# Gated delta rule in a decoder kernel: smaller TensorE tiles for the triangular inverse and the output, and eight steps in flight for five

## The chip, the cores and the metric

The kernel runs on one core of a Trainium2 chip, as one launch. The metric is the device time of that launch in microseconds (us). All data are float32. The engines are named as the profile names them: PE is TensorE's matmul, PEld its weight load, DVE is VectorE, ACT is ScalarE, POOL is GpSimd, SP is SyncE, which here issues DMAs.

## What is computed

A decoder of two layers works on 32 sequences of 64 tokens, 256 wide. Layer 0 has a decaying linear attention, a windowed cross attention and a feed-forward part; layer 1 has a gated delta rule, a cross attention and a mixture of 64 experts. The change lies in the delta rule alone. Cut to its core, with one chunk of 64 tokens per sequence (so that the running state of the reference is zero and drops out):

```
q, k, v   = silu(causal conv over 4 tokens of x @ w_qkv)      # 16 key heads, 32 value heads, 128 wide
q, k      = l2norm(q) * 128**-0.5, l2norm(k)
decay     = where(lower, exp(g_i - g_j), 0)
A         = where(strict, -(beta * k) @ k.T * decay, 0)       # 64 x 64 per sequence and head
T         = inverse of (I - A)                                # unit lower triangular
o         = where(lower, q @ k.T * decay, 0) @ (T @ (beta * v))
x         = x + (rmsnorm(o) * norm_w * silu(x @ w_z)) @ w_out
```

## The kernel before, in words

The delta rule is the stage in lines 711 to 1205. It works in 64 steps: 16 key heads by 4 groups of 8 sequences (512 tokens). Each step has two value heads, so 16 matrices A of 64x64. They lie in tiles of 128 partitions by 8 units by 64: two sequences on the two halves of the partitions, and eight units (four token tiles by two heads) along the free dimension.

A step s is made by these generators, each a stream of its own:

- `conv` (line 831): the projection pp (line 850), the causal convolution as one ACT and three DVE instructions (lines 854 and 859), and silu (864). It runs four times a step, for k, q and two halves of v.
- `decay` (867): one broadcast load per two steps, two POOL subtractions and additions per step, one exp.
- `matrices` (892): squares on POOL (903), their sums pn on PE (910), the products pk (943), and the masked matrices am (A transposed) and at (attention transposed) on DVE (951). It stores am to a DRAM buffer adram (957) and, for every second step, loads the 16x16 diagonal blocks from it as w, 512 blocks on 128 partitions by four (964).
- `value` (972): transposes v on PE (985) and scales it on ACT (989).
- `invert` (996): inverts the 16x16 blocks of two steps on DVE with 28 small instructions (1007, 1010), stores the inverses and their transposes in the DRAM buffer tudram (1016), and loads them as tu (1028): T and its transpose U, 64x64 with the four 16x16 diagonal blocks filled.
- `delta` (1055): completes the inverse in two levels, from blocks of 16 to 32 and from 32 to 64. First level: px = A T (am as the weights) on the left columns of each pair of blocks, a masked copy into xi (1085), ptu = T xi (U as the weights), a copy back into T (1090). Second level: a second px, and pm = T^T at (both in line 1067), a masked copy into the second xi (1097), a copy of pm to mt (1100), a last pm = xi^T mt for the right half, and its copy (1105). The helper `per_sequence` (1063) issues one 64x64 matmul per unit and sequence, so 16 in a block.
- `output` (1108): po, values times mt (1118), 16 matmuls with 64 rows and 128 weight columns; the square on ACT, the gate on DVE, the sum of squares pso on PE (1136), and the inverse root on POOL (1144).
- `gate` (1035): pz (1047) and silu. `project` (1148): py (1158), scaled and added to x on ACT, DVE and POOL (1165, 1167, 1169).

The order is written by a planner, `scheduled` (line 41). Each stream yields the engine and the time that it expects of its next piece; the planner takes the piece that could start first, and among those within 0.3 us of it the one whose stream stands first in the list (lines 1187 to 1195). "need" and "set" order pieces in the plan: conv needs the step five or six before to be done, and invert the step two pairs before. The number behind a stream is how many of its items may be open. "+" takes one of six PSUM banks, "-" gives it back, "c" means the two banks of conv, "t" a small tile shape. The plan fixes the order on every engine; the waits that the chip then makes come from the data and the buffers.

Of the kernel before, what the change touches and what calls it, by code (L numbers as in the profile page):

```python
# [23 lines left out]
LEVELS = (16, 32)  # L24
# [96 lines left out]
def decoder_kernel(ctx: ExitStack, tc: tile.TileContext, d, out):  # L121
# [589 lines left out]
    with tc.tile_pool(name="g1", bufs=1) as wp, tc.tile_pool(  # L711
# [6 lines left out]
        id64 = load(wp, d["c_id64"], [P, S], "id64")  # L718
        low = load(wp, d["c_low"], [P, S], "low")
        lvl = wp.tile([P, 2, S], U8, name="lvl")  # L720
# [4 lines left out]
        adram = [dp.tile([2, 2, 8, PITCH], FP, name=f"adram{i}") for i in range(2)]  # L725
        tudram = [dp.tile([2, 2, 2, 8, PITCH], FP, name=f"tudram{i}") for i in range(2)]
# [4 lines left out]
        xis = [[wp.tile([P, 8, S], FP, name=f"xi{l}{i}") for i in range(2)] for l in range(2)]  # L731
        for i in range(2):
            nc.sync.dma_start(out=wo16[i].rearrange("p o j e -> p o (j e)"), in_=d["c_wid"].rearrange("p (o x) -> p o x", o=2))
        for xs_ in xis:
            for t in xs_:
                nc.gpsimd.tensor_copy(t, over(id64, 8))
# [10 lines left out]
        with tc.tile_pool(name="g1l", bufs=1) as tmp:  # L747
            lvlf = load(tmp, d["c_lvl"].rearrange("p (l i) -> p l i", l=2), [P, 2, S], "lvlf")
# [68 lines left out]
        seqs = [slice(64 * n, 64 * n + 64) for n in range(2)]  # L817


        def load_weights(kh):  # L820
            wqkv = sb.tile([P, 2, 4, P], FP, name="wqkv", tag="wqkv")
            for i, at, n in ((0, kh, 1), (1, 16 + kh, 1), (2, 32 + 2 * kh, 2)):
                nc.sync.dma_start(
                    out=wqkv[:, :, i : i + n, :].rearrange("p k n e -> p k (n e)"),
                    in_=wsrc[:, :, at * P : (at + n) * P],
                )
            wz = load(sb, zsrc[:, :, kh * 256 : (kh + 1) * 256], [P, 2, 256], "wz")
            wo = load(sb, osrc[:, 2 * kh : 2 * kh + 2, :], [P, 2, D], "wo")
            weights[kh] = wqkv, wz, wo

        def conv(s, i):
# [3 lines left out]
            if i == first:  # L835
                yield "need", ("done", s - (5 if i == 2 or c == 0 else 6))
# [18 lines left out]
            yield "dve", 2.3, "-"  # L855
# [36 lines left out]
        def matrices(s):  # L892
# [55 lines left out]
            am = sb.tile([P, 8, S], FP, name="am", tag="am", bufs=6)  # L948
            at = sb.tile([P, 8, S], FP, name="at", tag="at", bufs=6)
# [6 lines left out]
            for n in range(2):  # L956
                nc.sync.dma_start(
                    out=adram[m % 2][j, n, :, : 64 * S].rearrange("u (r e) -> r u e", e=S), in_=am[seqs[n]]
# [3 lines left out]
            if j:  # L962
                w = sb.tile([P, 16, 16], FP, name="w", tag="w")
                nc.sync.dma_start(
                    out=w,
                    in_=adram[m % 2].rearrange("c n u (b x) -> (c n u b) x", b=4)[:, : 16 * S]
# [29 lines left out]
        def invert(m):  # L996
# [3 lines left out]
            yield "need", ("done", 2 * m - 4)  # L1000
# [14 lines left out]
            for o in range(2):  # L1015
                nc.sync.dma_start(
                    out=tudram[m % 2][o].rearrange("c n u (b x) -> (c n u b) x", b=4)[:, : 16 * S]
# [4 lines left out]
            for j in range(2):  # L1022
                yield "need", ("stored", m)
                yield "need", ("done", 2 * m + j - 4)
                tu = sb.tile([P, 2, 8, S], FP, name="tu", tag="tu", bufs=4)
                for n in range(2):
                    for o in range(2):
                        nc.sync.dma_start(
                            out=tu[seqs[n], o],
                            in_=tudram[m % 2][o, j, n, :, : 64 * S].rearrange("u (r e) -> r u e", e=S),  # L1030
# [24 lines left out]
        def delta(s):  # L1055

            kh, c = steps[s]
            yield "need", ("inverse", s)
            am, at = tokens.pop(s)
# [3 lines left out]
            def per_sequence(dst, lhsT, rhs):  # L1063

                for u in range(8):
                    for n in seqs:
                        nc.tensor.matmul(dst[n, u], lhsT[n, u], rhs[n, u], start=True, stop=True)  # L1067

            def columns(m, l):

                return m.rearrange("p u (b two c) -> p u b two c", two=2, c=LEVELS[l])[:, :, :, 0]

            def units(name, l):
                t = ps.tile([P, 8, S // 2], FP, name=name, tag="ps")
                return t.rearrange("p u (b c) -> p u b c", c=LEVELS[l])
# [5 lines left out]
            yield "pe", 0.65, "+t"  # L1081
            px = units("px", 0)
            per_sequence(px, am, columns(T, 0))
            yield "dve", 0.45, "-"
            nc.vector.copy_predicated(columns(xi[0], 0), columns(over(lvl[:, 0, :], 8), 0), px)
            yield "pe", 0.65, "+t"
            pt = units("ptu", 0)
            per_sequence(pt, U, columns(xi[0], 0))
            yield "act", 0.45, "-"
            nc.scalar.copy(columns(T, 0), pt)  # L1090
            yield "pe", 1.6, "++t"
            px = units("px", 1)
            per_sequence(px, am, columns(T, 1))
            pm = ps.tile([P, 8, S], FP, name="pm", tag="ps")
            per_sequence(pm, T, at)
            yield "dve", 0.45, "-"
            nc.vector.copy_predicated(columns(xi[1], 1), columns(over(lvl[:, 1, :], 8), 1), px)
# [3 lines left out]
            yield "pe", 0.65, "+t"  # L1101
            pm = ps.tile([P, 8, S // 2], FP, name="pm2", tag="ps")
            per_sequence(pm, xi[1], mt[:, :, S // 2 :])
            yield "act", 0.45, "-"
            nc.scalar.copy(mt[:, :, S // 2 :], pm)
            yield "set", ("weights", s)

        def output(s):

            yield "need", ("weights", s)  # L1110
            yield "need", ("gate", s)
            yield "need", ("value", s)
            mt, vs, eo = outs.pop(s), values.pop(s), factors.pop(s)[1]
            yield "pe", 1.0, "++t"
# [399 lines left out]
```

## Time and profile before

| | us |
|---|---|
| median of 8 runs | 3693.08 |
| lowest, highest | 3685.01, 3703.21 |
| the profiled execution | 3688.37 |
| its span, first to last instruction | 3686.7 |
| the stage: first pp (line 850) to end of last py (line 1158) | 934.1 to about 2597 |
| PE busy in the whole span | 3361.7 |
| mean granted clock of TensorE | 0.935 |

A line of the time line has the start, the length, the engine, the source line, the operation, the tiles (output, then inputs), the shape of the array part in rows by columns, the partitions and columns of the output, the type, and how many records are merged in it. Behind it, in brackets, stands the idle time before it and what ended it. A matmul of fp32 leaves two records. A record is longer than the distance to the next, since matmuls overlap; a block's price is the distance from its start to the start of the next block. A line of the waits has who waited for whom, the sum in us, how often, and the longest. A line of the stretches has the length, and for PE, PEld, DVE, ACT and POOL the busy time and the number of instructions, then the granted clock, the share of the DMA engines and GB/s. The time line and the stretches count from the start of the span.

### The profile page before, as it was taken

How to read it: one execution, taken by the hardware profiler on the slowest of the kernel's cores; microseconds unless marked ns; L12 is line 12 of the kernel's file. 1: busy time of each engine (PE TensorE's matmuls, PEld its weight loads, DVE VectorE, ACT ScalarE, POOL GpSimd, SP SyncE). 2: the span in 40 equal slices, each digit the busy share in tenths (PEclk: the TensorE clock that was granted, in tenths of full speed). 3: DMA queues.
4: the chain of work that ended last, by engine and by line, in shares of the span. 5: the costliest groups of instructions: out<-in, count | busy, mean ns of one | idle time of the engine just before them, and what ended most of it. 6: DMA issues, size and time to landing. Idle time of an engine off the chain costs nothing.

```text
span 3686.7 us, 91942 instructions
## 1 busy us (share of the span) xinstructions
PE 3361.7 (91%) x39042; PEld 2154.1 (58%) x39042; DVE 2102.5 (57%) x4316; ACT 1383.0 (38%) x2422; POOL 1522.7 (41%) x1779
## 2 busy tenths in 40 slices
PE   9999999897799999999999999999788888599990
PEld 4667566565376666666666666767444444355550
DVE  4333555544667577676677677676555555233337
ACT  1110333321545455554555555464222222233330
POOL 3321344443434344433444444443233334466663
PEclk9999999997899899998999999999878878799995
DMA  9910111001323233332332323332111111466655
GB/s 311 385 27 15 41 33 33 21 28 37 83 51 69 45 67 64 62 68 50 63 56 55 73 55 66 68 56 44 43 43 47 41 40 39 135 211 215 217 177 214
DMA packets 538699, 317.80 MB, mean 86 GB/s; under 512 B 420144, under 2 KB 498736, under 8 KB 531888
## 3 DMA queue, kind: packets, MB, share of 16 engines
q1 hardware_dynamic: 517680, 259.32, 27.2%
q0 software_dynamic: 18432, 50.49, 3.7%
q8 instruction: 308, 5.05, 0.6%
q10 hardware_dynamic: 2176, 2.10, 0.2%
q14 instruction: 103, 0.84, 0.1%
HBM read 166.42 MB, written 137.00 MB: 82 GB/s over the span
## 4 chain that ended last, share of the span: by engine, by line
PE 75%; DVE 9%; issue 6%; POOL 5%; ACT 3%; DMA 1%; SPq 1%; another core or an unknown queue 1%; POOLq 0%; DVEq 0%; ACTq 0%
PE pp L850 11%; PE py L1158 6%; PE po L531 6%; PE pz L1047 5%; PE pq L296 4%; PE sc L467 4%; PE pm L1067 4%; PE sc L499 3%; PE px L1067 3%; PE po L1118 3%; PE py L384 3%; PE py L1372 3%; PE pg L1362 2%; PE pu L1362 2%; PE ptu L1067 2%
## 5 line engine op out<-in xcount | busy, mean ns | idle before, releaser
L859 DVE SCALAR_TENSOR_TENSOR acc<-pp,cw,acc 128x504 f32<-128x504 f32 (+2 forms) x768 | 556.6, 730 | 193.6 <-ACT acc L854 186.2
L850 PE MATMUL pp<-xT,wqkv 128*128 128x512 f32 x1024 | 507.6, 621 | 21.4 <-DMA wqkv<-in_w_qkv_dram 11.3
L509 ACT ACTIVATE eT<-sc 128x768 f32<-128x768 f32 (+1 forms) x256 | 222.3, 914 | 339.4 <-PE sc L499 223.5
L477 DVE TENSOR_REDUCE mext<-sc 128x4 f32<-128x768 f32 (+1 forms) x256 | 267.4, 1087 | 95.7 <-PE sc L467 66.0
L204 POOL DMA_INDIRECT ybuf<-ye,xe x256 | 245.5, 959 | 175.5 <-DVE ye L1376 95.7
L903 POOL TENSOR_TENSOR sq<-kq 128x512 f32<-128x512 f32 x128 | 134.1, 1050 | 441.4 <-ACT kq L864 334.9
L850 PEld LDWEIGHTS pp<-xT,wqkv 128*128 128x128 f32 x1024 | 186.5, 195 | 185.9 <-issue 168.7
L1169 POOL TENSOR_TENSOR x<-x,y 128x256 f32<-128x256 f32 x256 | 184.2, 726 | 256.8 <-DVE x L1167 250.2
L467 PE MATMUL sc<-k,q 32*128 32x192 f32 (+1 forms) x2048 | 214.5, 421 | 59.1 <-issue 49.2
L854 ACT ACTIVATE acc<-pp,cw 128x512 f32<-128x512 f32 x256 | 175.3, 686 | 238.0 <-PE pp L850 237.4
L1158 PE MATMUL py<-wo,og 128*128 128x256 f32 x1024 | 259.7, 392 | 2.3 <-DVE x L1167 2.3
L1047 PE MATMUL pz<-xT,wz 128*128 128x512 f32 x512 | 246.1, 601 | 0.0
L1158 PEld LDWEIGHTS py<-wo,og 128*128 128x128 f32 x1024 | 186.2, 192 | 43.6 <-issue 16.5
L518 POOL TENSOR_SCALAR_AFFINE_SELECT eT<-eT 128x256 f32<-128x256 f32 (+1 forms) x256 | 127.2, 532 | 201.4 <-ACT eT L509 201.4
L467 PEld LDWEIGHTS sc<-k,q 32*128 32x128 f32 x2048 | 123.4, 202 | 116.4 <-issue 90.9
L531 PE MATMUL po<-eT,va 128*32 128x192 f32 (+1 forms) x2048 | 183.1, 398 | 6.6 <-issue 3.4
L1365 DVE TENSOR_TENSOR hT<-hT,pu 96x512 f32<-96x512 f32 x64 | 43.7, 683 | 237.0 <-PE pu L1362 224.9
L499 PE MATMUL sc<-qb,k 32*128 32x192 f32 (+1 forms) x2048 | 165.6, 387 | 13.3 <-DVE mext L477 10.1
L531 PE MATMUL po<-eT,one 128*32 128x192 f32 (+1 forms) x2048 | 175.2, 386 | 2.5 <-issue 2.4
L1167 DVE SCALAR_TENSOR_TENSOR x<-py,ro,x 128x256 f32<-128x256 f32 x256 | 122.4, 480 | 95.4 <-ACT y L1165 93.5
L1144 POOL TENSOR_TENSOR ro<-gvar,mhalf 128x8 f32<-128x8 f32 x64 | 105.3, 1645 | 145.4 <-DVE gvar L1139 138.3
L1165 ACT ACTIVATE y<-py,ro 128x256 f32<-128x256 f32 x256 | 120.4, 472 | 113.1 <-PE py L1158 105.2
(226 smaller groups left out, 6513.5 us busy)
## 6 DMA issues: line engine op xcount, KB each, us to landing
xbuf<-zero SPq DMA_DIRECT2D x32, 1032.0 KB
xe<-xbuf SPq DMA_DIRECT2D x64, 516.0 KB
tu<-tudram SPq DMA_DIRECT2D x256, 128.0 KB
ybuf<-zero SPq DMA_DIRECT2D x16, 1024.0 KB
de<-gdram SPq DMA_DIRECT2D x64, 256.0 KB
adram<-am SPq DMA_DIRECT2D x128, 128.0 KB
yk<-ybuf SPq DMA_DIRECT2D x16, 1024.0 KB
kk<-kT SPq DMA_DIRECT2D x32, 256.0 KB
```

Source lines behind the costliest of these rows:

```text
L204: i = nc.gpsimd.indirect_dma_start(out=dst, out_offset=bass.IndirectOffsetOnAxis(ap=rows, axis=0), in_=src, in_offset=None).ins
L467: nc.tensor.matmul(sc[ng // 2][:, ng % 2, qt * W : (qt + 1) * W], q32[rows, r, qt * P : (qt + 1) * P], k32[rows, r, lo[qt] : lo[qt] + W], ...
L477: nc.vector.tensor_reduce(mv4[:, 2 * hf : 2 * hf + 2, :, 8], sc[hf][:, :, : 2 * W].rearrange("p j (q l) -> p j q l", l=W), AX.X, ALU.max, ...
L499: nc.tensor.matmul(sc[ng // 2][:, ng % 2, lt * W : (lt + 1) * W], k32[rows, r, lt * P : (lt + 1) * P], qb[rows, lo[lt] : lo[lt] + W], star ...
L509: nc.scalar.activation(eT[:, 2 * hf : 2 * hf + 2].rearrange("p j h q -> p j (h q)"), sc[hf][:, :, : 2 * W], AF.Exp, scale=float(1 / np.sqr ...
L531: nc.tensor.matmul(po[32 * ng : 32 * ng + 32, i, lo[lt] : lo[lt] + W], one8[:, r, :] if i else va[:, lt, ng, 32 * r : 32 * r + 32], eT[:, ...
L850: nc.tensor.matmul(pp, weights[kh][0][:, k, i, :], xT[c][:, k, :], start=k == 0, stop=k == 1)
L859: nc.vector.scalar_tensor_tensor(acc3[:, :, sh:], pp3[:, :, : S - sh], w[:, 3 - sh : 4 - sh], acc3[:, :, sh:], ALU.mult, ALU.add,)
L1047: nc.tensor.matmul(pz, weights[kh][1][:, k, h * P : (h + 1) * P], xT[c][:, k, :], start=k == 0, stop=k == 1)
L1067: nc.tensor.matmul(dst[n, u], lhsT[n, u], rhs[n, u], start=True, stop=True)
L1158: nc.tensor.matmul(py[:, h, :], og[:, 4 * h + t].rearrange("p n i -> p (n i)"), won[:, h, :], start=True, stop=True,)
L1169: nc.gpsimd.tensor_tensor(xt, xt, y1, ALU.add)
```

## The change

It has these parts, all in the delta-rule stage:

- First level: the matmuls of px and ptu work on the 32x32 diagonal blocks, so 32 matmuls of 32x32 by 16 columns replace 16 of 64x64 by 32. tu holds the two 32x32 diagonal blocks only ([128, 2, 8, 32]) and is loaded by eight DMAs a step in place of four.
- Second level and T^T at: the second px (16 matmuls of 32x32 by 32 columns) and pm (32 of 32x32 by 64) are issued in turns in one block. The second xi is filled by two plain copies of 32 partitions, one on DVE and one on ACT. The last pm has 16 matmuls with 32 weight columns in place of 64, and its result is copied by DVE and ACT, 32 partitions each.
- Output: 32 matmuls of 64x64 in place of 16 of 64x128.
- Depth: conv needs the step eight before; invert the step three pairs before; adram and tudram have three buffers, tu six, am and at eight, the weights three. Three new "need" entries: delta after the output of three steps before, output after the projection of two before, and the load of w after the store of two pairs before.
- Planner: other expected times for delta, output, conv and the inverse root; project and gate go down in the list of streams, invert goes up.

The core of the diff:

```diff
-                yield "need", ("done", s - (5 if i == 2 or c == 0 else 6))
+                yield "need", ("done", s - 8)
...
-            yield "need", ("done", 2 * m - 4)
+            yield "need", ("done", 2 * m - 6)
...
-                yield "need", ("done", 2 * m + j - 4)
-                tu = sb.tile([P, 2, 8, S], FP, name="tu", tag="tu", bufs=4)
-                for n in range(2):
-                    for o in range(2):
+                yield "need", ("done", 2 * m + j - 6)
+                tu = sb.tile([P, 2, 8, 32], FP, name="tu", tag="tu", bufs=6)
+                for o in range(2):
+                    for q in range(4):
+                        half = slice(32 * (q % 2), 32 * (q % 2) + 32)
                         nc.sync.dma_start(
-                            out=tu[seqs[n], o],
-                            in_=tudram[m % 2][o, j, n, :, : 64 * S].rearrange("u (r e) -> r u e", e=S),
+                            out=tu[quads[q], o],
+                            in_=tudram[m % 3][o, j, q // 2, :, : 64 * S].rearrange("u (r e) -> r u e", e=S)[half, :, half],
                         )
...
+            yield "need", ("output", s - 3)
...
-            def per_sequence(dst, lhsT, rhs):
+            def per_block(dst, lhsT, rhs):
                 for u in range(8):
-                    for n in seqs:
-                        nc.tensor.matmul(dst[n, u], lhsT[n, u], rhs[n, u], start=True, stop=True)
+                    for q, rows in enumerate(quads):
+                        w = lhsT[rows, u]
+                        if w.shape[-1] == S:
+                            w = w[:, 32 * (q % 2) : 32 * (q % 2) + 32]
+                        nc.tensor.matmul(dst[rows, u], w, rhs[rows, u], start=True, stop=True)
...
-            px = units("px", 1)
-            per_sequence(px, am, columns(T, 1))
-            pm = ps.tile([P, 8, S], FP, name="pm", tag="ps")
-            per_sequence(pm, T, at)
+            px, pm = units("px2", 32), units("pm", S)
+            for u in range(8):
+                for q, rows in enumerate(quads):
+                    if q % 2 == 0:
+                        nc.tensor.matmul(px[quads[q + 1], u], am[rows, u, 32:], T[rows, u], start=True, stop=True)
+                    nc.tensor.matmul(pm[rows, u], T[rows, u], at[rows, u], start=True, stop=True)
-            nc.vector.copy_predicated(columns(xi[1], 1), columns(over(lvl[:, 1, :], 8), 1), px)
+            nc.vector.tensor_copy(xi[1][quads[1]], px[quads[1]])
+            nc.scalar.copy(xi[1][quads[3]], px[quads[3]])
...
-            per_sequence(pm, xi[1], mt[:, :, S // 2 :])
-            nc.scalar.copy(mt[:, :, S // 2 :], pm)
+            for u in range(8):
+                for n in range(2):
+                    nc.tensor.matmul(
+                        pm[quads[2 * n], u], xi[1][seqs[n], u], mt[seqs[n], u, 32:], start=True, stop=True
+                    )
+            nc.vector.tensor_copy(mt[quads[0], :, 32:], pm[quads[0]])
+            nc.scalar.copy(mt[quads[2], :, 32:], pm[quads[2]])
...
+            yield "need", ("done", s - 2)
...
                 for n in range(2):
-                    nc.tensor.matmul(
-                        po[n][:, u % 2 * 4 + u // 2, :], vs[seqs[n], u, :], mt[seqs[n], u, :], start=True, stop=True
-                    )
+                    for dv in seqs:
+                        nc.tensor.matmul(
+                            po[n][dv, u % 2 * 4 + u // 2, :], vs[seqs[n], u, dv], mt[seqs[n], u, :],
+                            start=True, stop=True,
+                        )
...
-                ((project(s, t2) for s in each for t2 in range(2)), 2),
                 ((delta(s) for s in each), 2),
                 ((decay(m) for m in range(NS // 2)), 1),
+                ((project(s, t2) for s in each for t2 in range(2)), 2),
                 (convs(), 2),
+                ((invert(m) for m in range(NS // 2)), 1),
                 ((gate(s, h) for s in each for h in range(2)), 1),
-                ((invert(m) for m in range(NS // 2)), 1),
```

## The prediction, as it stood before the result was known

> **What bounds the kernel now.** I read the page first, then the stretches, the time line of TensorE in the delta-rule stage, its waits, and last the two programs' instruction orders.
>
> The page's busy line and chain:
>
> ```profile
> PE 3361.7 (91%) x39042; PEld 2154.1 (58%) x39042; DVE 2102.5 (57%) x4316; ACT 1383.0 (38%) x2422; POOL 1522.7 (41%) x1779
> PE 75%; DVE 9%; issue 6%; POOL 5%; ACT 3%; DMA 1%; SPq 1%; another core or an unknown queue 1%; POOLq 0%; DVEq 0%; ACTq 0%
> ```
>
> TensorE is nearly always busy and is three quarters of the chain. A busy PE need not be PE at its peak, so I look at the stage itself. The time line puts its first convolution (line 850) at 934 us and its last projection (line 1158) at 2597: 1663 us for 64 steps, 26.0 us a step. In stretches (busy time of PE, PEld, DVE, ACT, POOL; granted clock; DMA):
>
> ```profile
> 1100.00:1400.00 300.00, 291.94 (x4216) 198.09 (x4216) 207.20 (x478) 156.37 (x280) 119.72 (x123) 0.96 0.31 60
> 2000.00:2300.00 300.00, 298.32 (x4441) 200.73 (x4440) 220.78 (x521) 168.75 (x300) 132.23 (x135) 1.00 0.32 63
> ```
>
> From 1100 to 2550 PE is busy 1433 of 1450 us, DVE 1026 (71%), ACT 772 (53%), POOL 613 (42%). So what PE's blocks cost is what the stage costs. The waits of PE in these 1450 us are short; the longest entry is:
>
> ```profile
> PE ptu L1067 <- DVE xi L1085: 6.5, 4, 2.8
> ```
>
> Now the price of each block, as the distance from its start to the next block's start where the clock is full:
>
> ```profile
> 1503.12 0.71 PE L910 MATMUL pn<-ones,sq 128*32 128x1 f32 x64
> 1503.77 1.98 PE L1047 MATMUL pz<-xT,wz 128*128 128x512 f32 x4
> ...
> 1526.84 1.12 PE L1067 MATMUL ptu<-xi,tu 64*64 64x32 f32 x32
> 1527.89 1.98 PE L1047 MATMUL pz<-xT,wz 128*128 128x512 f32 x4
> 1529.81 1.12 PE L1067 MATMUL px<-tu,am 64*64 64x32 f32 x32
> 1530.76 1.13 PE L1067 MATMUL pm<-at,tu 64*64 64x64 f32 x32
> 1531.82 0.66 PE L985 MATMUL pv<-ident,vv 128*128 128x128 f32 x4
> ...
> 1535.00 1.12 PE L1067 MATMUL pm<-mt,xi 64*64 64x32 f32 x32
> 1536.06 1.12 PE L850 MATMUL pp<-xT,wqkv 128*128 128x512 f32 x2
> 1537.11 2.00 PE L1118 MATMUL po<-mt,vs 64*128 64x64 f32 x32
> 1539.04 1.12 PE L1067 MATMUL pm<-mt,xi 64*64 64x32 f32 x32
> ```
>
> Each fp32 matmul leaves two records, so x32 is 16 matmuls. The prices: first level px 0.98 (a pair of px blocks is 1.98 elsewhere), ptu 1.05, second px 0.95, T^T at (pm) 1.06, last pm 1.06, output po 1.93; together 7.03 us of the 26. Per record that is 30 to 33 ns in 64x64 tiles and 60 ns in 64x128. The untouched rest is pp 4 x 1.81, pz 2 x 1.81, py 4 x about 0.9, pv 2 x 0.49, pn and pso 0.65 each, pk 1.03: 17.7. The sum, 24.7 x 64 = 1583 us, falls 80 short of 1663: PE's gaps and the stretches at half clock. In 1100 to 2550 the gaps are 17 us, and the clock stands at 0.5 for 63 us in nine stretches, most beginning at a gap of 0.8 us or more: 32 us lost.
>
> **The change, part by part.** The sum is made against the profiled execution, 3688.4 us (its span 3686.7 and 1.7 around it); the median of the eight runs, 3693.1, lies 4.7 above, and I add that at the end.
>
> *Output in 64x64 tiles*: 32 matmuls (64 records) for 16. The trace has this shape: scores of the first attention, 64x64 tiles, 64 columns, all four tiles taken in turn, each row half with a bank of its own, as in the new output.
>
> ```profile
> 75.73 2.10 PE L344 MATMUL pss<-qT,kk 64*64 64x64 f32 x128
> 77.75 1.98 PE L296 MATMUL pq<-xT,wq 128*128 128x512 f32 x4
> ```
>
> 2.02 us / 128 = 15.8 ns; x 64 = 1.01. I take 1.05, as a block next to another shape costs up to 0.1 more (ptu 1.05, px 0.95): 0.88 saved.
>
> *First level in 32x32 tiles*: px and ptu become 32 matmuls (64 records) of 16 columns each. Low end: pn, 64 records with 32 weight columns in four tiles, 0.65 us (10 ns). High end: each record keeps today's 32 ns, 2.05 us. The nearest row is pss, whose tiles differ in rows as well as columns (pn's all use the same 128 rows), but it has twice the weight columns. I take 14 ns, a little below its 15.8: 0.9 each, so 0.08 + 0.15 saved.
>
> *Second level and T^T at in turns*: 16 + 32 matmuls, 96 records, all in 32x32 tiles, for 2.01 us. At pn's price 0.96, at pss's 1.5, at 32 ns 3.07. I take 1.2: T^T at now uses four tiles at 64 columns, and today's pm shows that 64 columns in two tiles cost hardly more than 32 (33 against 30 ns). 0.81 saved.
>
> *Last pm*: still 32 records, now 32 weight columns. pn's 40 ns per tile (4 x 10) over two tiles gives 20 ns, 0.64; unchanged is 1.06. I take 0.7: 0.35 saved.
>
> Together 0.88 + 0.23 + 0.81 + 0.35 = 2.27 us a step, x 64 = **145 us**. Ends: 3.12 (200 us saved) at pn's price, and minus 2.25 (144 us lost) at today's price per record.
>
> [...]
>
> *Copies*. xi and mt halves go to DVE and ACT in pieces of 32 partitions. DVE loses two copy_predicated (432 and 441 ns) and gains one of half the width and two copies of 32x256. Nothing shows 32 partitions; between 0.16 (the shortest DVE row, ssum) and 0.44 each, at 0.3 DVE is unchanged (ends -0.4, +0.45). ACT: two copies of 371 ns become three, of which one has half the width: +0.3. Both hide under PE: DVE's 0.71 x 26.0 = 18.4 us a step is then 78% of 23.7, ACT 60%.
>
> *Moved and added DMA*. Per step SP issues eight tu loads of 32 KB for four of 128 KB; an issue takes 0.63 us now, so up to 2.5 us a step on SP, which has about ten issues (6 us) in 26. Behind them on SP wait the next am stores and weight loads. The longer lead hides it: the adram, tudram and tu buffers go from 2, 2 and 4 to 3, 3 and 6, and the am and at buffers from 6 to 8. Without that cover PE would wait 2.5 us wherever it has no other block; nothing to 20 us, I take 0. A third zero store of 1 MB stands on SP's queue before the loads of tri and wba, which line 770 waits for: the two now are issued at 886.4 and line 770 starts at 895.1, so 0 to +5, I take +4.
>
> *Eight in flight*. The two orders show less than the words: the first output follows 48 convolution matmuls in both, and at the 32nd output 292 have been issued for 280, so 1.5 steps more, not 3. It can win back the gaps and half-clock stretches, 49 us at most. The four waits of ptu for DVE, after which px stands close by, are still in the order. A faster PE also needs its fillers sooner. I take -8; ends -40 and +75 (below).
>
> *New waits*. Output now needs the projection of two steps before, and delta the output three before; these bound the planner, and the og and mt buffers (2 and 3) already did. Priorities move inversion ahead of the gate and delta ahead of projection: nothing queues behind that which is not in the order above. I take 0.
>
> **Sum**: 3688.4 - 145 + 4 - 8 = 3539; plus 4.7 and rounded: **3545**, own range 3510 to 3590.
>
> **Rivals.**
>
> *Records keep their price (slower).* If a record in 32x32 tiles costs 32 ns as in 64x64, then px 2.05 + ptu 2.05 + second block 3.07 + pm 1.06 + po 1.05 = 9.3 against 7.03: +2.25 x 64 = +144, and with 3688.4 and 4.7 about 3837. It decides from 24 ns a record: 224 records have 4.04 us today plus 1.23 saved on po and pm, 5.27 / 224. For it: the 32*128 scores of line 467 cost 59 ns a record with four row tiles, so row tiles alone win little there. Against it: pn's 10 and pss's 15.8.
>
> *PE becomes faster and then waits.* The chain of delta has five hops between PE and DVE or ACT, DVE is busier, and PSUM stays at six banks. At gaps of 4% in place of 1% in 1500 us, 45 us, and half-clock stretches growing alike, 30 us: 3545 + 75 = 3620. For it: DVE at 78%, the ptu waits. Against: 17 us of gaps in 1450 now.
>
> *Records at pn's price.* 200 us saved in place of 145, and the gaps as now: 3688.4 - 200 + 4 + 4.7 = 3497; with half of the 49 us won back too, 3473.
>
> *The change does not do what it says*: the depth indeed does little. Without the tiles' gain it would be a matter of gaps alone, within 0.2%, which is about what a measurement of this kernel can tell from no change.
>
> **How the numbers follow.** Forecast 0.60; faster waits 0.13; pn's price 0.12; no change 0.03; slower 0.12. Faster by over 0.2%: 0.60 + 0.13 + 0.12 = 0.85; within 0.2%: 0.03; slower: 0.12. The range 3470 to 3630 takes in the forecast, pn's price and most of the waiting case, and leaves out some 0.17.
>
> **What would show it.** In the changed profile's time line: po to next start 1.0 to 1.1; px and ptu 0.65 to 1.05; the block of px and pm in turns 1.0 to 1.5; last pm about 0.7. In its stretches: PE busy above 97% inside the stage, DVE near 78%, the stage about 1510 us long. I am wrong if the 32x32 records lie near 24 ns or above, or if PE's gaps in the stage pass 50 us with ptu waiting for xi or px for the loads of tu.

## The result, and the profile after

The change made the kernel slower: the changed kernel takes 3707.8 us (median of 13 runs), the kernel before 3693.2 (36 runs). The ratio is 1.0041, 95% interval 1.0032 to 1.0050. The forecast was 3545, some 163 us too low, and its range (3470 to 3630) does not hold the time.

The page of the changed kernel, its busy line and its chain of waits:

```profile
PE 3262.9 (88%) x47234; PEld 2020.5 (54%) x47234; DVE 2125.4 (57%) x4380; ACT 1389.4 (37%) x2486; POOL 1526.8 (41%) x1779
PE 64%; DVE 15%; issue 9%; POOL 5%; ACT 3%; DMA 2%; another core or an unknown queue 1%; SPq 0%; POOLq 0%; DVEq 0%; ACTq 0%
```

PE has 8192 more records and is busy for 99 us less, yet its span grew from 3686.7 to 3710.4. PE's share of the chain fell from 75% to 64%; DVE and "issue" took it. In the stage, two stretches (columns as in the prediction):

```profile
1100.00:1400.00 300.00, 276.57 (x5823) 177.34 (x5823) 211.04 (x500) 159.72 (x292) 123.97 (x127) 0.90 0.28 50
2000.00:2300.00 300.00, 275.50 (x6027) 174.36 (x6026) 214.62 (x500) 161.40 (x298) 130.98 (x133) 0.94 0.27 51
```

PE is now idle for 8% of the time in place of 1 to 3%, and the clock is lower. DVE, ACT and POOL are about as busy as before (211 us of the first 300 for DVE, 207 then): the work of a step got shorter for PE alone, and the step did not. The longest waits of PE in the stage (us in total, times, longest):

```profile
PE pm L1101 <- issue: 26.0, 22, 3.3
PE ptu L1075 <- issue: 23.5, 18, 3.9
PE pp L850 <- DVE acc L859: 18.7, 16, 3.3
PE px L1100 <- issue: 13.7, 11, 2.4
```

"issue" means that the engine waited for nothing that the profile shows. In the kernel before, the longest such entry of the stage is:

```profile
PE ptu L1067 <- issue: 2.4, 2, 1.5
```

In the changed kernel these waits stand in front of the small matmuls, and the time line of PE shows them inside blocks:

```profile
1527.46 1.16 PE L1134 MATMUL po<-mt,vs 64*64 64x64 f32 x64
1528.55 1.09 PE L943 MATMUL pk<-kq 128*64 128x128 f32 x16
...
1533.47 0.73 PE L1075 MATMUL px<-tu,am 32*32 32x16 f32 x64
1534.13 0.71 PE L1153 MATMUL pso<-ones,osq 128*32 128x1 f32 x64
1537.32 1.05 PE L1075 MATMUL px<-tu,am 32*32 32x16 f32 x64 [2.48 <-DVE cj L924]
1538.16 1.06 PE L1075 MATMUL ptu<-xi,tu 32*32 32x16 f32 x63
1541.14 0.23 PE L1075 MATMUL ptu<-xi,tu 32*32 32x16 f32 x1 [1.92 <-issue]
```

Three things are to be seen. First, the blocks cost what was hoped or less: po to pk 1.09, px to pso 0.66. Second, ptu stops between its 63rd and 64th record, where no data can be missing. Third, 64 + 63 = 127 records lie between that stop and the one ahead of px, put down to cj, which belongs to another step's decay and not to px. After the first stop the same px takes 1.05 in place of 0.73: the granted clock is 0.5 from 1536.8 to 1547.1 us. The count holds in the whole stage: 75 waits of PE have no releaser, and from one to the next it is 126 to 128 records in 36 of 74 cases, and about a multiple of 127 (254, 381, 508) in most of the others.

Records come in pieces. A record of a matmul has one of a weight load beside it (39042 of each on the page before, 47234 on the page after), and the page counts the transfers of instructions, in packets of 16 KB (packets, MB, share of 16 engines' span); before and after:

```profile
q8 instruction: 308, 5.05, 0.6%
```

```profile
q8 instruction: 372, 6.09, 0.7%
```

64 more packets for 8192 more records is 128 records a packet. In the transfers of that queue by time, packets begin at 1534.60 and 1538.88, 2.7 and 2.3 us ahead of the two ends of stops above. No two of them begin less than 3.3 us apart anywhere in that trace.

The stage, added up from the trace (first pp to end of last py; "work" is an estimate, the length less PE's idle time and half of the time at half clock: blocks of the changed kernel that lie whole at half clock took 3.68 us for four records of pp, at full clock 1.81, but 0.98 for 64 of px in 32x32 tiles, at full clock 0.66, so it counts somewhat too much clock against the small tiles; a stop is idle time of over 0.15 us that ends 2.0 to 3.3 us after a 16 KB transfer began, so some other waits fall in by chance):

| us | length | idle | of it stops | at half clock | work |
|---|---|---|---|---|---|
| before | 1663.3 | 31.5 | 3.8 (3 stops) | 89.6 | 1586.9 |
| after | 1682.6 | 152.1 | 102.2 (81 stops) | 265.6 | 1397.6 |

So 189 us of PE's work went away, and 121 us of idle time and (265.6 - 89.6) / 2 = 88 us of slow clock came: +19 in all. Of the 102 us of stops, 93 have no releaser.

The stages behind the delta rule took 975 to 989 us in some rounds of runs and 1081 to 1092 in others, whatever the kernel, so each run below is told as a ratio to the kernel before in the same round, with its 95% interval, and the stage's parts come from its own profile.

### The profile page after: what moved, and what is told of

Read it like the earlier page. It is cut to its first block, busy times and chain, and to the rows that moved or that the text cites. A ratio compares the mean times of both kernels' runs of the same rounds, so it can differ in the third digit from the quotient of the medians.

```text
span 3710.4 us, 108769 instructions
## 1 busy us (share of the span) xinstructions
PE 3262.9 (88%) x47234; PEld 2020.5 (54%) x47234; DVE 2125.4 (57%) x4380; ACT 1389.4 (37%) x2486; POOL 1526.8 (41%) x1779
## 4 chain that ended last, share of the span: by engine, by line
PE 64%; DVE 15%; issue 9%; POOL 5%; ACT 3%; DMA 2%; another core or an unknown queue 1%; SPq 0%; POOLq 0%; DVEq 0%; ACTq 0%
PE pp L850 8%; PE po L530 5%; PE py L1175 5%; DVE acc L859 4%; PE pq L295 4%; PE sc L466 4%; PE pz L1050 4%; PE sc L498 3%; PE py L1389 3%; PE pg L1379 2%; PE pu L1379 2%; PE py L383 2%; DVE wtmp L1008 2%; DVE w L1011 2%; PE pk L943 2%
## 5 line engine op out<-in xcount | busy, mean ns | idle before, releaser
L1175 PE MATMUL py<-wo,og 128*128 128x256 f32 x1024 | 288.9, 421 | 4.7 <-issue 3.3
L1175 PEld LDWEIGHTS py<-wo,og 128*128 128x128 f32 x1024 | 199.4, 207 | 50.6 <-issue 20.9
L1182 ACT ACTIVATE y<-py,ro 128x256 f32<-128x256 f32 x256 | 118.6, 473 | 102.5 <-PE py L1175 92.1
L297 DVE TENSOR_TENSOR tmp<-pq,cs 128x1024 f32<-128x1024 f32 x80 | 98.0, 1225 | 100.3 <-PE pq L295 95.4
```

What stands on the lines that cost most here:

```text
L1175: nc.tensor.matmul(py[:, h, :], og[:, 4 * h + t].rearrange("p n i -> p (n i)"), won[:, h, :], start=True, stop=True,)
```

## Theories

**A, instructions.** PE's instructions arrive in pieces of 128 records, one in about 3.6 us (an estimate from the changed kernel, whose packets begin 3.3 us apart or more and whose stops follow one another 3.5 us apart or more). Matmuls in four 32x32 tiles take 10 ns a record (px, 0.66 us for 64), so a run of them uses up a piece in 1.3 us and PE stops; the stops bring the clock down. **B, the chain.** PE waits for DVE, ACT and the loads of tu, as the prediction's waiting case had it. **C, the order.** Eight steps in flight or the new priorities cost time by themselves.

Sixteen runs follow. The table has the fifteen with a stage of their own, in us as above; the sixteenth, bursts, adds work behind the stage.

| run | ratio | length | idle | stops | half clock | work |
|---|---|---|---|---|---|---|
| after_again | 1.0030 (1.0010, 1.0050) | 1677.9 | 150.2 | 98.0 | 261.2 | 1397.0 |
| after_spread | 0.9882 (0.9853, 0.9911) | 1606.8 | 100.7 | 27.0 | 100.6 | 1455.8 |
| before_spread | 1.0044 (1.0029, 1.0060) | 1680.4 | 33.6 | 1.9 | 35.7 | 1628.9 |
| after_fewer | 1.0320 (1.0291, 1.0349) | 1766.1 | 92.5 | 55.2 | 272.6 | 1537.3 |
| before_split | 1.0080, a single run | 1690.7 | 32.7 | 10.8 | 103.7 | 1606.2 |
| tiles_d5 | 0.9962 (0.9938, 0.9987) | 1644.5 | 138.7 | 70.3 | 192.7 | 1409.5 |
| d5_spread | 0.9919 (0.9894, 0.9945) | 1632.6 | 119.4 | 54.7 | 134.6 | 1445.9 |
| depth8 | 1.0112 (1.0088, 1.0135) | 1701.6 | 61.4 | 7.9 | 112.0 | 1584.2 |
| prio | 1.0094 (1.0060, 1.0127) | 1694.2 | 47.5 | 6.9 | 127.8 | 1582.8 |
| depth8_oldprio | 1.0106 (1.0079, 1.0132) | 1698.2 | 58.8 | 4.4 | 118.6 | 1580.2 |
| after_oldprio | 0.9957 (0.9940, 0.9975) | 1631.2 | 127.9 | 69.9 | 165.7 | 1420.4 |
| output64 | 0.9869 (0.9835, 0.9903) | 1617.6 | 40.0 | 10.5 | 86.8 | 1534.2 |
| lean1 | 0.9946 (0.9927, 0.9966) | 1636.9 | 61.6 | 9.0 | 124.0 | 1513.3 |
| lean2 | 0.9846 (0.9825, 0.9866) | 1609.1 | 90.0 | 43.1 | 113.0 | 1462.6 |
| lean2_s06 | 0.9902 (0.9879, 0.9925) | 1617.4 | 73.4 | 17.1 | 80.5 | 1503.8 |

## Experiments on the supply of instructions

**bursts**: the kernel before, and behind the stage three bursts whose results nothing uses: 512 matmuls of one column in four tiles (the shape of pn), 16 of 128x128 by 512, and 512 in 64x64 tiles.

```diff
+        for r in range(512):
+            rows = slice(32 * (r % 4), 32 * (r % 4) + 32)
+            nc.tensor.matmul(pa[rows, r // 4 % 16 : r // 4 % 16 + 1], bw[:, 32 * (r % 16) : 32 * (r % 16) + 32], ones[:, 0:1], start=True, stop=True)
+        for r in range(16):
+            nc.tensor.matmul(pb, bw[:, :P], xT[1][:, 0, :], start=True, stop=True)
+        for r in range(512):
+            n = seqs[r % 2]
+            nc.tensor.matmul(pd[n, r // 2 % 8], bw[n, 64 * (r // 2 % 8) : 64 * (r // 2 % 8) + 64], xT[1][n, 0, :32], start=True, stop=True)
```

> The kernel before with three bursts on PE behind the delta-rule stage, whose results are not used: 512 matmuls of 128x32 tiles with one column (1024 records), 16 matmuls of 128x128 with 512 columns, 512 matmuls of 64x64 tiles with 32 columns (1024 records). Instruction blocks: the first burst passes 128 records in not less than 3.5 us, so 8 x 3.5 = 28 us, 27 ns a record, though pn's blocks show 10 ns; the third at its own 30 ns a record, 31 us, without stops. Both rivals: the first burst takes 1024 x 10 ns = 10 us.

Its time line, PE alone:

```profile
2590.97 2.19 PE L1204 MATMUL pa<-ones,bw 128*32 128x1 f32 x242
2595.53 1.89 PE L1204 MATMUL pa<-ones,bw 128*32 128x1 f32 x128 [2.37 <-issue]
2599.55 1.89 PE L1204 MATMUL pa<-ones,bw 128*32 128x1 f32 x128 [2.13 <-issue]
2603.29 1.89 PE L1204 MATMUL pa<-ones,bw 128*32 128x1 f32 x128 [1.86 <-issue]
2607.04 1.89 PE L1204 MATMUL pa<-ones,bw 128*32 128x1 f32 x128 [1.86 <-issue]
...
2618.59 16.70 PE L1207 MATMUL pb<-xT,bw 128*128 128x512 f32 x32
2635.22 30.05 PE L1211 MATMUL pd<-xT,bw 64*64 64x32 f32 x1024
```

242 records run through (that these had been fetched ahead is an inference of mine); then exactly 128 come at a time, every 3.74 us from the third piece on, with 1.86 us of stop, and there is no data to wait for. That is 29 ns a record sustained, where the first 242 took 9 ns each. The whole burst took 27.6 us, as theory A had it (28), against 10 by both rivals. The granted clock is 0.5 from 2593.4 us, just inside the first stop, to 2624.1, so 1.9 us of each 3.74 are the records at half clock and the rest is the stop. The burst in 64x64 tiles, 30.05 us / 1024 = 29 ns a record by its own length, has no stop: that shape ran no faster than the 29 ns at which the pieces came. This shows theory A's stops by themselves, and agrees with the kernel before, whose 64x64 tiles at 30 ns met 3.8 us of them.

**after_spread** and **before_spread**: the same matmuls, but the planner is told that a small-tile block directly after another small-tile block costs 1.0 us more (in place of 0.1 us for each change between small and large), so it lays the blocks apart.

```diff
-            if engine == "pe" and ("t" in flags) != ("t" in mode[0]):
-                t += 0.1
+            if engine == "pe" and "t" in flags and "t" in mode[0]:
+                t += 1.0
```

> The changed kernel, but the planner adds 1.0 us to the start of a small-tile block that would follow another small-tile block, so that wide blocks (pp, pz, py, pv) come between. Theory, instruction blocks: in the changed kernel PE stops at every 127th or 128th record inside runs of small matmuls, each time until 2.3 to 2.9 us after a 16 KB transfer began on the instruction queue, and such stops follow one another 3.5 us or more apart; 81 of them take 102 us, and the clock stands at half for 268 us in place of 90 after them. Spread out, the stops should fall to about 25 us and the half clock to about 130 us: 3707 - 75 - 70 = about 3560 (3530 to 3620). Rival, clock by tile size: the small tiles themselves lower the clock: stops shrink, half clock stays near 268 us, 3630 or more. Rival, order and depth: the new priorities and the depth make PE wait for DVE and ACT: not below 3690.

> The kernel before, tiles and depth untouched, with the spreading rule alone. Instruction blocks: it has only about 4 us of such stops, so nothing to win; changing tile shape more often costs some 0.1 us a block: 1.000 to 1.020 of the kernel before. If the rule simply makes a better order for DVE and ACT, it is faster here too, 0.985 or less, and the spread run proves nothing on instruction blocks.

On the changed kernel this wins, as theory A expected, but by less: 0.9882, where the changed kernel has 1.003 to 1.004 and 3560 us would have been 0.964. The stops fall from 102 to 27 us (25 forecast) and half clock from 266 to 101 (130 forecast). What the forecast left out is the price: 58 us more work and 24 us more of idle time that is no stop. The time alone would suit the rival of clock by tile size; that rival had half clock staying near 268, and it did not. The waits of PE without a releaser in that kernel's stage, the longest three:

```profile
PE ptu L1075 <- issue: 8.8, 4, 3.2
PE px L1075 <- issue: 5.7, 5, 2.4
PE pm L1101 <- issue: 4.6, 8, 1.3
```

pm's 26.0 us have become 4.6. On the kernel before the same rule loses, 1.0044: there were hardly any stops to take away (3.8 us). So it is no better order in general; it helps where small records stand in runs. Half clock fell there too, from 90 to 36 us, so not all of its fall on the changed kernel need come from the stops. The rule has a price in both: PE's work grows by 42 us (before) and 58 (after). The number of changes between small and large tile shapes goes from 8.7 to 12.6 a step, and from 9.8 to 14.0; each costs some 0.1 us in the blocks' prices (a pp block of the kernel before costs 1.72 us between two wide blocks, 1.81 to 1.82 with a small one on one side, and 1.91 between two small ones, medians at full clock), which I estimate at about 26 us for 260 changes; the rest of the price is not traced.

**after_fewer**: the changed kernel with pn and pso as 8 matmuls of 128 weight columns each in place of 32 of 32, so 96 records a step fewer.

```diff
-                for q4 in range(4):
-                    rows = slice(32 * q4, 32 * q4 + 32)
-                    nc.tensor.matmul(pso[rows, u : u + 1], tok[:, rows], ones[:, 0:1], start=True, stop=True)
+                nc.tensor.matmul(pso[:, u : u + 1], tok, ones[:, 0:1], start=True, stop=True)
```

> The changed kernel with the sums pn and pso made by 8 matmuls of 128 weight columns in place of 32 of 32 each: 416 records a step for 512, the same results. By po's 60 ns a record for 128 weight columns the two blocks cost about 0.95 us each in place of 0.65, +40 us in all. Instruction blocks: stops 102 to about 45 us, half-clock loss 45 us less: 3707 + 40 - 57 - 45 = 3645 (3600 to 3690). Both rivals: the 40 us are simply added, about 3747.

It lost 3.2%, where theory A had 0.987 and its rivals 1.015. Two lines of its time line:

```profile
1507.80 1.84 PE L1148 MATMUL pso<-ones,osq 128*128 128x1 f32 x16
1509.51 1.93 PE L908 MATMUL pn<-ones,sq 128*128 128x1 f32 x16
```

1.71 us for 16 records is 107 ns each, where 60 had been assumed, so pn and pso got dearer by about 2.1 us a step, 135 us. The stops fell by nearly half (55.2 us, where A had about 45), but the half-clock time did not fall. The clock rows suggest why: 19 of this run's 39 stretches at half clock have no gap of over 0.5 us in the 3.5 us ahead of them, and each of the 19 has one of the new pn or pso blocks there, though only 37% of the stage lies that close behind one. In the changed kernel none of 35 is without such a gap. So this run seems to have brought a second way to lose the clock, and it does not test the first.

**before_split**: the kernel before, with pp's 512 columns cut in four, so 48 records a step more with no new small tile.

```diff
-            for k in range(2):
-                nc.tensor.matmul(pp, weights[kh][0][:, k, i, :], xT[c][:, k, :], start=k == 0, stop=k == 1)
+            for cc in range(4):
+                cols = slice(P * cc, P * cc + P)
+                for k in range(2):
+                    nc.tensor.matmul(pp[:, cols], weights[kh][0][:, k, i, :], xT[c][:, k, cols], start=k == 0, stop=k == 1)
```

> The kernel before with each 512-column matmul of the convolutions cut into four of 128 columns: 432 records a step for 384, but the added ones lie in wide blocks, where a record lasts some 110 ns. Instruction blocks as runs that are too fast: the stops stay at about 4 us. If the mere number of instructions costs: as many stops as with the output's 416 records, 10 us or more.

The stops came to 10.8 us by the count of the table, which is the rival's mark (10 or more). But 6.1 of them are two waits of ptu for xi, which fall in by chance; without a releaser there are 3.8 us, as in the kernel before. The entries of its waits:

```profile
PE ptu L1069 <- DVE xi L1087: 9.4, 5, 4.0
PE ptu L1069 <- issue: 3.2, 2, 1.7
```

So 48 records a step more in wide blocks bring no stops: what counts is how closely the records stand, not their number alone.

## Experiments on the depth and the order

**tiles_d5** has the changed tiles with the depth, buffers, needs and priorities of the kernel before; **d5_spread** adds the planner's rule to it; **after_again** is the changed kernel again, in the round of the runs beside it.

```diff
-                yield "need", ("done", s - 8)
+                yield "need", ("done", s - (5 if i == 2 or c == 0 else 6))
```

> All the new tiles (first level, second level with T^T at, output) with depth, buffers, added needs and priorities as before the change. Instruction blocks: still 512 records a step, so stops and half clock as in the changed kernel: 3690 to 3730. Order and depth as the cause: the tiles' gain shows, about 3560. Clock by tile size: as the changed kernel.

> The changed kernel itself, to have it beside the others on one chip. Every theory: 1.004 of the kernel before (1.000 to 1.010); stage of the delta rule 1683 us, with PE's gaps near 150 us and half clock near 265 us in it.

> All the new tiles, depth, needs and priorities as before the change, and the spreading rule of the planner (1.0 us against a small-tile block behind another). Instruction blocks: stops about 25 us as in the spread kernel with the changed depth (0.988 of the kernel before); the depth adds nothing: 0.980 to 0.990. If depth or priorities cost by themselves, clearly below 0.985; if the depth is what keeps PE fed between wide blocks, above 0.992.

The tiles alone win 0.4% where the changed kernel loses 0.3 to 0.4%; theory A had expected no difference. So it does not hold all of it: the other half of the change costs some 0.7%. Spreading helps here too (55 against 70 us of stops, 0.9919 against 0.9962), less than on the changed kernel and less than expected (0.980 to 0.990).

**depth8** has the old tiles with eight in flight, its buffers, its needs and the priorities (the weights and tu keep their buffers, for lack of memory, and the first step of each key head needs the fifth before). **prio** has the new priorities alone, **depth8_oldprio** the depth with its buffers and needs but the old priorities, **after_oldprio** the changed kernel with the old priorities.

The edit of prio, whose reverse makes after_oldprio:

```diff
-                ((project(s, t2) for s in each for t2 in range(2)), 2),
                 ((delta(s) for s in each), 2),
                 ((decay(m) for m in range(NS // 2)), 1),
+                ((project(s, t2) for s in each for t2 in range(2)), 2),
                 (convs(), 2),
+                ((invert(m) for m in range(NS // 2)), 1),
                 ((gate(s, h) for s in each for h in range(2)), 1),
-                ((invert(m) for m in range(NS // 2)), 1),
```

> The kernel before with the old tiles and the depth, added needs and priorities of the change; am, at, adram and tudram have the new numbers of buffers, tu and the weights the old ones, for want of room, so the first convolutions of a key head stay at five steps. Instruction blocks: no more than 10 us of stops, since the records stay at 384 a step with 30 ns in the long runs: 0.995 to 1.003. If order and depth cost by themselves: 1.01 or more.

> The kernel before with the changed kernel's priorities of the streams alone; five steps in flight, old tiles, old buffers. The run with eight steps in flight and old tiles cost 1.1%, with few stops for instructions (7.9 us). If the priorities make that cost, this run has a ratio of 1.007 to 1.012 against the kernel before. If the depth makes it, 0.998 to 1.003, with PE's idle time in the stage near the 31 us of the kernel before.

> Old tiles, eight steps in flight with their buffers, but the priorities of the kernel before. If the depth by itself costs, the ratio stays at 1.008 to 1.013. If the priorities cost, it is 0.997 to 1.003. In between, both have a part.

> The changed kernel with the priorities of the kernel before. If PE's stops for instructions set its time, it is the order of small matmuls that counts: laid out by 3.6 us for every 128 records, this order is short of 93 us where the changed kernel's is short of 142, so some 50 us and the clock behind them go: ratio 0.980 to 0.992. If the priorities made no difference to the stops, 1.000 to 1.005 as the changed kernel.

I had expected depth8 to be level. It is not, and on the old tiles depth and priorities each cost about 1% alone and 1.1% together: the costs do not add, and neither is the one culprit. The stops are 4 to 8 us in all three, so this is not theory A. It is idle time (16 to 30 us more) and clock: PE's waits in depth8_oldprio name what came late:

```profile
PE pp L850 <- DVE acc L859: 13.7, 18, 1.7
PE pn L910 <- POOL sq L903: 11.7, 9, 2.4
PE pp L850 <- DVE wtmp L1008: 8.7, 3, 3.6
```

Waits on DVE's acc, POOL's sq and DVE's wtmp are 4.7, 4.8 and 3.3 us in the kernel before: PE's next convolution comes before DVE has done the one ahead of it, or pn before POOL's squares. On the new tiles the depth costs nothing that can be told (after_oldprio 0.9957, tiles_d5 0.9962), while the new priorities cost 0.7% (after_again 1.0030): with them the stops go from 70 to 98 us and the half-clock time from 166 to 261. So there theories A and C meet: the same matmuls in the order of the new priorities stop more often. The gain, 0.7%, is less than the 1.2% or more that the order alone had promised. (Depth and its three needs were not tried apart, nor the planner's new expected times, which the runs with the new tiles of the change have and those with old tiles have not.) Theory B has a part in the changed kernel, and a small one: idle time that is no stop rose from 28 to 50 us in its stage.

## Experiments on single tiles

**output64**: the kernel before with po alone in 64x64 tiles. **lean1**: that, and the last pm with 32 weight columns. **lean2**: lean1, and the second level and T^T at in turns in 32x32 tiles. The first level stays in 64x64, and the depth at five. **lean2_s06**: lean2 with a spread of 0.6 us in the planner.

```diff
-                    nc.tensor.matmul(
-                        po[n][:, u % 2 * 4 + u // 2, :], vs[seqs[n], u, :], mt[seqs[n], u, :], start=True, stop=True
-                    )
+                    for dv in seqs:
+                        nc.tensor.matmul(
+                            po[n][dv, u % 2 * 4 + u // 2, :], vs[seqs[n], u, dv], mt[seqs[n], u, :],
+                            start=True, stop=True,
+                        )
```

lean1's addition, with the copy of the result by DVE and ACT as in the changed kernel:

```diff
-            per_sequence(pm, xi[1], mt[:, :, S // 2 :])
+            for u in range(8):
+                for n in range(2):
+                    nc.tensor.matmul(
+                        pm[quads[2 * n], u], xi[1][seqs[n], u, :32], mt[seqs[n], u, 32:], start=True, stop=True
+                    )
```

lean2's, with the two plain copies into xi:

```diff
-            per_sequence(px, am, columns(T, 1))
...
-            per_sequence(pm, T, at)
+            for u in range(8):
+                for q, rows in enumerate(quads):
+                    if q % 2 == 0:
+                        nc.tensor.matmul(px[quads[q + 1], u], am[rows, u, 32:], T[rows, u, :32], start=True, stop=True)
+                    nc.tensor.matmul(
+                        pm[rows, u], T[rows, u, 32 * (q % 2) : 32 * (q % 2) + 32], at[rows, u], start=True, stop=True
+                    )
```

> The kernel before with only the output in 64x64 tiles: 416 records a step for 384, the output's block 1.09 us for 1.93. Instruction blocks: few runs reach 128 records within 3.5 us, since px and its like stay at 30 ns a record, so the 54 us (0.84 x 64) are kept but for some 10: 0.986 to 0.990 of the kernel before. Clock by tile size: also about 0.987. Order and depth: 0.985.

> The kernel before with the output in 64x64 tiles and the last pm with 32 weight columns: 416 records a step as with the output alone (0.987 of the kernel before), but the last pm at 0.63 us for 1.05 to 1.06. Instruction blocks: no more stops than with the output alone, so its 27 us are kept: 0.979 to 0.984. Clock by tile size: the half clock grows with another small shape, 0.985 or more.

> As the one before, and second level with T^T at in turns in 32x32 tiles: 448 records a step, the pair of blocks about 1.35 us for 2.01, 42 us more saved. Instruction blocks: runs of second level, last pm and output now reach 128 records within 3.5 us at times; some 20 us of stops and 15 us of half clock come back: 0.974 to 0.984. Clock by tile size: above 0.985.

> Second level and T^T at in 32x32 in turns, first level and output in 64x64, five steps in flight, and the planner counts 0.6 us in place of 0.1 for a change of shape between small matmuls, which spreads their blocks. By 3.6 us for 128 records its order is short of 23 us where the same tiles without the spread are short of 49. If the stops for instructions rule, the ratio falls from 0.985 to 0.975 to 0.982. If spreading costs in waits for DVE and in order what it saves in stops, 0.983 to 0.992.

output64 gives 1.3% by itself: 53 us of PE's work gone (the forecast's 0.88 us x 64 = 56), and few stops (10.5 us, 5.0 of them without a releaser), with its records at 17 ns and 32 more a step. lean1, expected at 0.979 to 0.984, took 21 us more of work away and lost all of it and more (0.9946): idle 61.6 against 40.0, half clock 124 against 87, with stops at 9.0. That is not A: PE's longest waits without a releaser there (8.8 us ahead of ptu, in five) end 3.6 to 18 us after the last transfer of instructions began, where the stops of the table end within 3.3. Nor is it PE's work, which fell. It looks like an order with more waits, which was not tried by itself; a swing of nearly 1% by such things has to be reckoned with in every one of these rows. lean2 has the lowest ratio, **0.9846**, just short of its forecast (0.974 to 0.984), and its interval overlaps those of output64 and after_spread: 124 us of work gone, 58 us of idle time and 12 us of clock given back against the kernel before. It beats both the kernel before and the changed one. Its stretch from 1100 to 2550, ahead of that of the changed kernel:

```profile
1100.00:2550.00 1450.00, 1374.53 (x26465) 891.01 (x26462) 1082.82 (x2527) 802.15 (x1476) 633.46 (x651) 0.96 0.31 61
```

```profile
1100.00:2550.00 1450.00, 1327.78 (x28682) 847.00 (x28682) 1033.05 (x2401) 764.26 (x1418) 606.76 (x618) 0.92 0.27 49
```

PE is busier in lean2, with fewer records and a higher clock, and DVE, ACT and POOL do 4 to 5% more of their work in the same time: that is the step getting shorter. Spreading lean2 took 26 us of stops and 32 us of half clock away and cost 41 us of work: 0.9902, as the rival for that run had it (0.983 to 0.992).

## Why the prediction was wrong, point by point

- *What bounds the kernel*: right for the kernel before. PE's blocks set the stage, and output64's stage is 46 us shorter where its block lost 0.84 x 64 = 54. But the words ahead of the prediction, that the chip's waits come from the data and the buffers, leave out a third source: the instructions themselves (93 us of stops without a releaser in the changed kernel's stage).
- *Output in 64x64*, forecast 1.05: measured 1.09. *First level*, 0.9 each: 0.66, at pn's 10 ns a record, with four row tiles that write one bank, so 0.7 us a step saved in place of 0.23. *Second level in turns*, 1.2: 1.10 where nothing stops it. *Last pm*, 0.7: 0.63. The sum is 4.13 us in place of 7.03, 2.90 x 64 = 186 us where the forecast had 145 and the stage's work 189. The tiles did more than was forecast.
- *Copies and DMA at nothing*: in the stage DVE's busy time rose from 1165 to 1188 us and ACT's from 874 to 880, 0.4 and 0.1 us a step, and no wait of PE for a load of tu stands among the longest. Not tried by themselves.
- *Eight in flight, -8; new waits and priorities, 0.* Wrong. On the old tiles depth and priorities cost 1% each; on the new ones the priorities cost 0.7%, some 27 us. "Nothing queues behind that which is not in the order above" was said of data; how close the small matmuls come to stand was not looked at.
- **The step that failed** is the one from "what PE's blocks cost is what the stage costs" to the sum: it put PE's new idle time and slow clock at nothing (0 for DMA, waits and priorities, -8 for the depth), with no word on what feeds PE its instructions. The rival "PE becomes faster and then waits" priced waiting at 75 us. It came to 121 us of idle time and 88 us of clock, 209 in all, more than the 189 us of work saved, and most of the idle time (98 of 121) was not the wait for DVE or ACT that the rival had in mind, but the one for instructions. The tests named in the prediction say so: PE busy 92% between 1100 and 2550 where above 97% was asked, DVE 71% where 78%; gaps of 152 us where 50 was the limit, but ptu stood mostly without a releaser, not waiting for xi.
- *Records keep their price*, the slower rival, decided at 24 ns a record. In a block they cost 10 ns; in a long run 29 (pn's shape, run bursts), above that point. The rival looked for the price in the array, and it was in the supply. Its hint stood in the page of before: 308 instruction packets of 16 KB, which I did not divide by the records.

The size of a piece, 128 records of matmuls with their 128 weight loads, is the same by three counts: 64 packets of 16 KB for 8192 records, the 126 to 128 records between two waits in 36 of 74 cases, and the 128 of each piece in bursts. Its arrival is not hidden behind PE's work: pm, a block of small matmuls, waited up to 3.3 us without a releaser, and at px's 10 ns 128 records take 1.3 us.

Still open: what sets the 3.7 us of a piece (its transfer is recorded for 1.07 us, the median of the changed kernel's 372), why lean1 waits more than output64, how much of the half clock is the stops' alone, and how depth and priorities come to cost 1% each and no more together.

## What to carry to other kernels

Before cutting matmuls into smaller tiles, divide the time that the stage's densest run of matmul records will take by their number, and compare it with what bursts showed: 242 records ran through at 9 ns each, and from then on PE got 128 in 3.74 us, 29 ns a record, and stood for 1.86 us of that. Cut where a block's price falls and few stops come with it (the output: 1.3% and 10.5 us of stops for 32 more records a step), leave the others, and put large matmuls between the small ones as far as each change of shape (some 0.1 us here) pays. And test a planner's depth and priorities apart from the tiles: here either moved the time by 1% with the same instructions.

## What had not been expected of the hardware

- Instructions for PE come in pieces of 128 records, one in 3.74 us when PE uses them up, and 242 records ran through at the start of a burst (run bursts).
- In the changed kernel the granted clock falls to half behind short gaps. Between 1000 and 2550 us it has 33 such stretches, of 3.4 to 17.1 us; the kernel before has 11, three of them with no gap in the 7 us ahead. The longest gap close ahead of one of the 33 is 2.0 us in the median, 0.64 us at the least and 3.87 at the most, so the waits may cost nearly as much again in clock as in themselves: 88 us, by the estimate of half of the time at half clock, against 121. Not every gap does it: of 59 of over 0.8 us that began at full clock, 38 had half clock within 7 us.
- A matmul of fp32 with 128 weight columns and one column of data leaves two records of 107 ns each (run after_fewer), while one of 32 weight columns, four tiles in turn, leaves them at 10 (the changed kernel): for the same sums, 16 records took 1.71 us and 64 took 0.65. Behind such blocks lie 19 of after_fewer's 39 stretches at half clock, with no gap of over 0.5 us in the 3.5 us ahead of them.
